# A decoder's first layer on one core: the tile experts' silu written with tanh, and the order of a recurrence's exponentials, loads and scatters

## The chip, the core and the metric

The kernel runs on one core of one Trainium2 chip. A core has TensorE (PE, matrix products and transposes), VectorE (DVE), ScalarE (ACT), GpSimd (POOL) and SyncE (SP, which only issues DMAs here); each runs its own instructions in order and waits for the others by semaphores. Products land in PSUM, everything else lies in SBUF. The metric is the device time of one execution in microseconds (us), as the median of a few runs.

## The reference

A decoder of two layers on x of 16 sequences × 128 tokens × 256 channels, all float32. The change lies in layer 0 and in the early part of layer 1:

```python
x = x + L0_attn(layernorm(x))           # 16 heads of 128, causal
x = x + L0_xattn(k=layernorm(x), v=ctx) # recurrence over the 128 tokens, per channel
x = x + L0_ffn(layernorm(x))            # 16 experts, 4 per token, and a shared expert
x = x + L1_attn(layernorm(x))
x = x + L1_xattn(layernorm(x), ctx)
x = x + L1_ffn(layernorm(x))            # weights and activations rounded
```

The recurrence carries (aa, bb, pp) from token to token and has four exponentials per token:

```python
q = max(pp, u + k);   e1 = exp(pp - q);       e2 = exp(u + k - q)
y = (e1 * aa + e2 * v) / (e1 * bb + e2)
q2 = max(pp + w, k);  e1b = exp(pp + w - q2); e2b = exp(k - q2)
aa, bb, pp = e1b * aa + e2b * v, e1b * bb + e2b, q2
```

An expert is `(silu(h @ w_gate) * (h @ w_up)) @ w_down`, with silu(g) = g · sigmoid(g), which is also 0.5 · g · (1 + tanh(g / 2)).

## The kernel before

The work is laid out for PE, whose order is the program's own in the stages below. The other engines' instructions are ordered at build time by a scheduler; `tc.issue_after(ins)` adds an edge that puts what is issued under it behind `ins` on the engine of `ins`.

**Layer-0 attention, 0 to about 610 us.** 64 units, each four heads of one sequence; 16 units make a group g of four sequences. In each step, `pipeline` runs `scores` (products into `sc`, L587; ACT copies them scaled, L589; POOL masks, L590; then the softmax with its maxima on DVE, L187, and four exponentials on ACT, L190), `values` (L625), `ahead` (the next heads' projections `proj`, L577, read out by ACT as qT and kT, L579; in one step per group POOL also adds a bias row to all of a group's x, L570), `project_out` (L175), `turn` (transposes of the probabilities, copied as `probT`, L203) and `between`.

**The recurrence beside it.** When a group's attention is done, `wkv_and_route(g)` is queued as a generator. `between` advances it by `take` with a credit of 20 per unit; each `yield` states a cost (UNIT is 15, SMALL 3). `wkv` goes through two blocks k of 128 channels: a load of vT, the context's values (L285, 256 KB, on ACT's queue), running maxima on DVE, two exponentials e1b and e2b (L295, L298), running sums aa and bb by scans, two exponentials in place of pp and q (L312, L314), and the quotient, transposed back and added to x. `route` then takes the router's choices of the group: for each token and each of its four experts a row number, first as float `fidx` and then as integers `idx` (L520, one copy per group). The 16 scatters of a group (L527, indirect DMAs issued by POOL, each 128 rows) wait in a list; `some_scatters` issues them, two per unit.

**Shared expert, about 620 to 753 us.** 24 units of `sh_hidden`, `sh_down` and `advance`. `advance(u)` runs the last group's recurrence and routing (it has no attention beside it), then `tile_map` and the first two fetches, with the edge behind `sh_hidden.last`, the unit's DVE product. SP's queue here holds the loads of the shared expert's weights, then the experts' weights (`wbig`, `wd`).

**Experts, about 753 to 1016 us.** 79 tiles j of 128 rows. Step s: `fetch`, `turn_in(s-2)` (transpose `pht`, L954, copied to `hxT` by ACT), `inner(s-3)` (product `pgu`, L970, gate and up in one PSUM tile; silu on ACT, L975; times up on DVE, L977), `turn_act(s-5)` (`pat`, L984), `outer(s-6)` (`pey`, L993) and `beside(s)`. The four PSUM tiles of a step come from one pool of four. From s = FIRST = 36 on, every second step, `beside` issues pieces of layer 1's self attention from three tables, among them its exponentials (L1168).

Of the kernel before, what the change touches and what calls it, by code (L numbers as in the profile page):

```python
# [12 lines left out]
AF = mybir.ActivationFunctionType  # L13
ALU = mybir.AluOpType
# [3 lines left out]
P = 128  # L18
# [4 lines left out]
G = 4  # L23
NG = B // G
GT = G * S
# [6 lines left out]
IMOE = 176  # L32
# [20 lines left out]
def decoder(ctx, tc, a, out):  # L53
    nc = tc.nc
    V, A, PE, GP = nc.vector, nc.scalar, nc.tensor, nc.gpsimd
# [13 lines left out]
    def ps4(name, pool="main"):  # L69
        return pools[pool].tile([P, 4, P], F32, tag="ps", name=name)  # L70
# [113 lines left out]
    def softmax(pool, sc, p):  # L184

        nmax = pool.tile([P, 4], F32, tag="nmax", name="nmax", bufs=3)
        softmax.last = V.tensor_reduce(nmax, sc, AX.X, ALU.max, negate=True).ins  # L187
        rs = pool.tile([P, 4], F32, tag="rsum", name="rsum", bufs=4)
        for i in range(4):
            A.activation(p[:, i, :], sc[:, i, :], AF.Exp, bias=nmax[:, i : i + 1], accum_out=rs[:, i : i + 1])  # L190
        return rs

    def normalised(p, rs):
# [34 lines left out]
    def flat(v):  # L228
        return v.rearrange("p t s -> p (t s)")
# [16 lines left out]
    UNIT, SMALL = 15, 3  # L246

    def take(steps, credit, unit=UNIT):
# [7 lines left out]
                credit -= cost  # L256
        return min(credit, 0)

    def wkv(g, psum):

        if not wpad:
            with tc.issue_after(softmax.last):
                wkv.wneg = wkv_setup()
        wneg = wkv.wneg
        mv, rstd = norm_stats(wkp, g)
        kp = [wkp.tile([P, G, SP], F32, tag=f"kp{k}", name=f"kp{k}") for k in range(NK)]
        yield 6
        hs = norm_rows(wkp, g, mv, rstd)
        yield UNIT
        with tc.issue_after(behind[0]):  # L270
            norm_T(hs, lambda k: kp[k][:, :, 1:], psum)
        yield 3
        for k in range(NK):

            def padded(tag, first):
                r = wkp.tile([P, G, SP], F32, tag=tag, name=tag)
                if first is not None:
                    GP.memset(r[:, :, 0:1], first)
                return r, r[:, :, :S], r[:, :, 1:]

            def plain(tag):
                return wkp.tile([P, G, S], F32, tag=tag, name=tag)

            vT = plain("vT")
            nc.scalar.dma_start(flat(vT), a["ctxT"][k * P : (k + 1) * P, g * GT : (g + 1) * GT])  # L285
            GP.memset(kp[k][:, :, 0:1], NEG)
            kt = kp[k][:, :, 1:]
            u = tfirst[:, k : k + 1]
            pp, pp0, pp1 = padded("pp", None)
            V.tensor_tensor_scan(flat(pp), flat(wpad[k]), flat(kp[k]), NEG, ALU.add, ALU.max)  # L290
            yield 3

            e1b, e1b0, e1b1 = padded("e1b", 0.0)
            V.scalar_tensor_tensor(e1b1, pp0, wneg[:, k : k + 1], pp1, ALU.add, ALU.subtract)
            A.activation(e1b1, e1b1, AF.Exp)  # L295
            e2b, bb0, e2b1 = padded("e2b", 0.0)
            GP.tensor_tensor(e2b1, kt, pp1, ALU.subtract)
            A.activation(e2b1, e2b1, AF.Exp)  # L298
            yield 2
            ev, aa0, ev1 = padded("ev", 0.0)  # L300
            GP.tensor_tensor(ev1, e2b1, vT, ALU.mult)
            q = plain("q")
            V.scalar_tensor_tensor(q, kt, u, pp0, ALU.add, ALU.max)
            yield 13

            V.tensor_tensor_scan(flat(ev), flat(e1b), flat(ev), 0.0, ALU.mult, ALU.add)
            yield 3
            V.tensor_tensor_scan(flat(e2b), flat(e1b), flat(e2b), 0.0, ALU.mult, ALU.add)
            yield 3

            GP.tensor_tensor(pp0, pp0, q, ALU.subtract)
            A.activation(pp0, pp0, AF.Exp)  # L312
            V.scalar_tensor_tensor(q, kt, u, q, ALU.add, ALU.subtract)
            A.activation(q, q, AF.Exp)  # L314
            yield 10
            GP.tensor_tensor(vT, q, vT, ALU.mult)
            V.tensor_tensor(bb0, pp0, bb0, ALU.mult)
            yield 4
            V.tensor_tensor(bb0, bb0, q, ALU.add)
            yield 2  # L320
            V.tensor_tensor(aa0, pp0, aa0, ALU.mult)
            V.tensor_tensor(aa0, aa0, vT, ALU.add)
            yield 4
            for t in range(G):
                V.reciprocal(bb0[:, t], bb0[:, t])
                yield 3
            y = q
            V.tensor_tensor(y, aa0, bb0, ALU.mult)
            yield UNIT
            pb = ps4("addb", psum)  # L330
            with tc.issue_after(behind[0]):
                for t in range(G):
                    PE.transpose(pb[:, t, :], y[:, t, :], ident)
            cols = slice(k * P, (k + 1) * P)
            V.tensor_tensor(xg[g][:, :, cols], xg[g][:, :, cols], pb, ALU.add)
            yield 3
# [8 lines left out]
    idx = rt.tile([P, B, TOPK], I32, name="idx")  # L345
# [63 lines left out]
    def route(g, psum):  # L409
# [8 lines left out]
        tiles = slice(g * G, (g + 1) * G)  # L418
# [21 lines left out]
        nmax = small("rmax", [P, G])  # L440
# [5 lines left out]
        rs = small("rrs", [P, G])  # L446
# [55 lines left out]
        for t in range(G):  # L502
            b = g * G + t
# [13 lines left out]
        V.tensor_tensor(both, pick, over_k(place_), ALU.mult)  # L517
        fidx = small("fidx", [P, G, TOPK])
        V.tensor_reduce(fidx, both, AX.X, ALU.add)
        V.tensor_copy(idx[:, tiles, :], fidx)  # L520
        yield SMALL
        V.tensor_tensor(both, pick, over_k(comb), ALU.mult)
        V.tensor_reduce(wts[:, tiles, :], both, AX.X, ALU.add)

        def scatter(t, k):
# [4 lines left out]
            tc.declare_no_dep(ins, group="hs", reason="no two tokens of an expert have one place")  # L530
            tc.add_to_no_dep_group("hs", ins)

        for t in range(G):
            for k in range(TOPK):
                scatters.append((scatter, t, k))
        yield SMALL

    def wkv_and_route(g, psum):
        yield from wkv(g, psum)
# [273 lines left out]
    def advance(u):  # L813

        behind[:] = last_pe
        with tc.issue_after(sh_hidden.last):
            advance.credit = take(steps, advance.credit, 10 if u % SHJ == 0 else 17)
        if u == 0:
            advance.power = power.last
        if u >= 2:  # L820
            some_scatters(4, advance.power)
# [137 lines left out]
    def inner(j):  # L959
        if j % NB == 0:  # L960
            _, vals = nc.values_load_multi_w_load_instructions(
                tmapT[0:1, 0, j : j + NB], engines=[ET], min_val=0, max_val=E - 1,
                skip_runtime_bounds_check_because=why,
            )
            for i, v in enumerate(vals):
                held[j + i] = v
        hT = live[j]
        pg = tps.tile([P, 2 * IMOE], F32, tag="t", name="pgu")
        for k in range(NK):
            PE.matmul(  # L970
                pg, hT[:, k, :], wgu[:, k, bass.ds(held[j], 1), :].rearrange("p e i -> p (e i)"),
                start=k == 0, stop=k == NK - 1,
            )
        s = mp.tile([P, IMOE], F32, tag="esilu", name="esilu", bufs=2)
        inner.last = A.activation(s, pg[:, :IMOE], AF.Silu).ins  # L975
        act = mp.tile([P, IMOE], F32, tag="eact", name="eact")
        softmax.last = V.tensor_tensor(act, s, pg[:, IMOE:], ALU.mult).ins  # L977
        live[j] = act

    def turn_act(j):  # L980
# [226 lines left out]
    early = ([(sa_out_T, 3)], [(sa_exponents, 4)], [(sa_values, 4)], [(sa_back, 4), (sa_norm_T, 6)])  # L1207
    late = ([(sa_project, 5), (sa_again, 4), (sa_out, 3)], [], [], [(sa_scores, 5)])
    last = ([(row_stats, 6)], [(sa_scale, 6)], [(sa_rows, 6), (sa_split, 5)], [])
# [3 lines left out]
    def pieces(table, u):  # L1213
        b, n = divmod(u, NKV)
        for f, ahead in table[n]:
            if 0 <= b + ahead < B - apart.get(f, 0):
                f(b + ahead)
# [22 lines left out]
    LAG, FIRST, APART = 6, 36, 2  # L1240
# [3 lines left out]
    def beside(s):  # L1244
        for _ in range(3):
            if s >= 1 and chores:
                chores.pop(0)()
        if s == FIRST + 6:
            assert not chores
            rawstack.close()  # L1250
            prepared()
        b, r = divmod(s - GATHER, TOPK)
        if r == 0 and 0 <= b < B - 2:
            back_rows(b)
        b, r = divmod(s - GATHER - 6, TOPK)
        if r == 0 and 0 <= b < B:
            back_sums(b)
        u, r = divmod(s - FIRST, APART)
        if r == 0 and 0 <= u < LEAD:
            u -= LEAD  # L1260
            for table in (early, late, last):
                pieces(table, u)
            for f, b, at in first_pieces:
                if u == at:
                    f(b)
        if s == NTILES + 2:
            load_weights()

# [395 lines left out]
```

## Time and profile before

| | |
|---|---|
| median of 3 runs | 1672.91 us (1672.89 to 1674.83) |
| profiled execution | 1670.1 us |
| its span, first to last instruction | 1668.4 us |
| mean granted clock of TensorE | 0.993 |
| ACT table loads: L723, L1168, L975 | 7, 4, 4 of 1283 ns each |
| vT loads, L285 | 8, issue 334 ns (median) |
| exponential of the recurrence, e.g. L314 | 128x512, 0.63 us |
| scatter, L527 | 64, 1009 ns mean |

A row of the profile names the line, the engine, the operation and the tile it writes "<-" those that it reads, then the shape. "Idle before <-releaser" tells how long the engine stood before the instruction and what ended that. A table load is ACT's change from one set of functions to another. PEld is PE's weight load, which runs beside its products. "remote" and "issue" stand where no instruction of the core is seen to have ended the wait.

### The profile page before, as it was taken

What the parts mean: (1) busy time and instruction counts of PE and PEld (TensorE: products, weight loads), DVE (VectorE), ACT (ScalarE), POOL (GpSimd) and SP (SyncE); (2) the same over time, 40 slices, a digit from 0 to 9 for tenths busy, and PEclk for the clock granted to TensorE, in tenths of its full rate; (3) what the DMA queues carried; (4) which work ended last, traced back from release to release, by engine and by line L of the source; (5) the groups of instructions that cost most, each with busy time, mean ns of one, the idle gap of its engine ahead of it and who ended that gap; (6) DMA issues with size and microseconds to landing.
All of it is one profiled execution on the core that took longest, in us unless ns stands there. A gap on an engine that the chain in (4) does not pass through costs nothing.

```text
span 1668.4 us, 27303 instructions
## 1 busy us (share of the span) xinstructions
PE 1615.0 (97%) x9808; PEld 1145.4 (69%) x9808; DVE 947.5 (57%) x2490; ACT 815.4 (49%) x2211; POOL 571.5 (34%) x586
## 2 busy tenths in 40 slices
PE   8999999999999989999999999999999999999997
PEld 4666666666666665656766667777777777777774
DVE  2333476457537656633354555567666666666756
ACT  3444454444445433303434445656666666665554
POOL 2010132144024233031364345654444444432331
PEclk9999999999999999999999999999999999999998
DMA  9990000000001028034443234000000000000000
GB/s 298 404 370 1 0 7 7 14 26 27 0 20 38 7 83 230 1 103 133 141 146 102 89 92 168 17 14 11 8 8 7 8 8 8 8 8 10 4 4 13
DMA packets 92205, 110.22 MB, mean 66 GB/s; under 512 B 8679, under 2 KB 67495, under 8 KB 92071
## 3 DMA queue, kind: packets, MB, share of 16 engines
q1 hardware_dynamic: 83638, 89.55, 16.5%
q0 software_dynamic: 6144, 16.79, 3.1%
q10 hardware_dynamic: 2288, 2.14, 0.4%
q8 instruction: 78, 1.28, 0.3%
q14 instruction: 57, 0.46, 0.1%
HBM read 54.06 MB, written 54.39 MB: 65 GB/s over the span
## 4 chain that ended last, share of the span: by engine, by line
PE 85%; DVE 6%; issue 3%; ACT 3%; POOL 2%; DMA 0%; SPq 0%; POOLq 0%; another core or an unknown queue 0%; DVEq 0%; ACTq 0%
PE proj L577 12%; PE acc_x L1433 6%; PE proj L1367 6%; PE acc_l L175 6%; PE projv L596 5%; PE pgu L970 5%; PE pey L993 4%; PE sc L1398 3%; PE z L1418 3%; PE sc L587 3%; PE z L625 3%; PE pg L717 2%; PE acc_sh L736 2%; PE pk L1333 2%; PE pu L717 2%
## 5 line engine op out<-in xcount | busy, mean ns | idle before, releaser
L190 ACT ACTIVATE sc<-sc,nmax 128x128 f32<-128x128 f32 x512 | 199.0, 390 | 162.2 <-DVE nmax L187 132.4
L187 DVE TENSOR_REDUCE nmax<-sc 128x4 f32<-128x512 f32 x128 | 87.3, 682 | 159.5 <-POOL sc L590 157.9
L590 POOL TENSOR_SCALAR_AFFINE_SELECT sc<-sc 128x512 f32<-128x512 f32 x64 | 42.1, 658 | 317.1 <-ACT sc L589 317.1
L1367 PEld LDWEIGHTS proj<-hc,wbig 128*128 128x128 f32 x1024 | 124.0, 192 | 29.2 <-issue 23.4
L125 POOL TENSOR_TENSOR rq<-rq,mhalf 128x4 f32<-128x4 f32 x64 | 67.8, 1059 | 210.4 <-DVE rq L1390 194.2
L577 PE MATMUL proj<-hT,wq 128*128 128x512 f32 x256 | 122.5, 601 | 4.3 <-DVE probT L203 3.9
L1433 PE MATMUL acc_x<-wbig,zT 128*128 128x256 f32 x512 | 124.6, 386 | 0.7 <-ACT zT L1424 0.7
L1367 PE MATMUL proj<-hc,wbig 128*128 128x128 f32 x1024 | 124.6, 275 | 0.1
L175 PEld LDWEIGHTS acc_l<-wo,zT 128*128 128x128 f32 x512 | 96.7, 190 | 36.8 <-issue 26.5
L577 PE MATMUL proj<-hT,wk 128*128 128x512 f32 x256 | 120.9, 595 | 0.0
L175 PE MATMUL acc_l<-wo,zT 128*128 128x256 f32 x512 | 120.9, 379 | 0.0
L596 PE MATMUL projv<-wv,hT 128*128 128x512 f32 x256 | 120.6, 593 | 0.0
L970 PE MATMUL pgu<-wbig,hxT 128*128 x316 | 109.0, 468 | 1.8 <-DVE eactT L986 0.5
L1433 PEld LDWEIGHTS acc_x<-wbig,zT 128*128 128x128 f32 x512 | 93.4, 190 | 24.0 <-issue 11.5
L125 POOL TENSOR_TENSOR ss<-ss,mhalf 128x32 f32<-128x32 f32 x16 | 87.6, 5477 | 45.0 <-DVE ss L1116 44.8
L1227 POOL DMA_INDIRECT back<-hs,idx x64 | 64.3, 1005 | 94.2 <-DMA hs<-ey 40.7
L190 ACT ACTIVATION_READ_ACCUMULATOR sc<-sc,nmax 128x1 f32 x512 | 95.6, 187 | 0.0
L1401 DVE SCALAR_TENSOR_TENSOR sc<-sc,rq,mask 128x128 f32<-128x128 f32 x256 | 77.5, 344 | 28.2 <-PE sc L1398 24.7
L577 PEld LDWEIGHTS proj<-hT,wk 128*128 128x128 f32 x256 | 49.1, 192 | 62.1 <-issue 53.2
L986 DVE COPY eactT<-pat 88x256 f32<-88x256 f32 x79 | 33.0, 418 | 101.4 <-PE pat L984 82.3
L625 PEld LDWEIGHTS z<-probT,v 128*128 128x128 f32 x512 | 66.9, 191 | 31.8 <-issue 27.0
L993 PE MATMUL pey<-wd,eactT 88*128 x316 | 82.0, 381 | 1.6 <-ACT hxT L956 0.9
(349 smaller groups left out, 3501.0 us busy)
## 6 DMA issues: line engine op xcount, KB each, us to landing
hs<-zero SPq DMA_DIRECT2D x16, 2048.0 KB
hx<-hs SPq DMA_DIRECT2D x79, 128.0 KB
hs<-ey SPq DMA_DIRECT2D x79, 128.0 KB
wbig<-in_L_ffn_w_gate_dram SPq DMA_DIRECT2D x2, 1408.0 KB
wbig<-in_L_ffn_w_up_dram SPq DMA_DIRECT2D x2, 1408.0 KB
wd<-in_L_ffn_w_down_dram SPq DMA_DIRECT2D x2, 1408.0 KB
wq<-in_L_attn_W_Q_dram SPq DMA_DIRECT2D x8, 256.0 KB
vT<-in_ctxT_dram ACTq DMA_DIRECT2D x8, 256.0 KB
```

Source lines behind the costliest of these rows:

```text
L125: power.last = GP.tensor_tensor(v, v, mhalf[:, :n], ALU.pow).ins
L175: ins = PE.matmul(acc[:, t, :], zT[:, i, :], w[:, h0 + i, :], start=h0 == 0 and i == 0 and t % 2 == 0, stop=last and i == 3, skip_group_ch ...
L187: softmax.last = V.tensor_reduce(nmax, sc, AX.X, ALU.max, negate=True).ins
L190: A.activation(p[:, i, :], sc[:, i, :], AF.Exp, bias=nmax[:, i : i + 1], accum_out=rs[:, i : i + 1])
L577: PE.matmul(pj, w[:, k, h, :], hTs[g][:, k, :], start=k == 0, stop=k == NK - 1)
L596: PE.matmul(pv, hTs[g][:, k, at], wv[:, k, 4 * hq : 4 * hq + 4, :].rearrange("p h e -> p (h e)"), start=k == 0, stop=k == NK - 1,)
L625: PE.matmul(pz[:, i, :], v[:, i, :], pT[:, i, :], start=True, stop=True)
L970: PE.matmul(pg, hT[:, k, :], wgu[:, k, bass.ds(held[j], 1), :].rearrange("p e i -> p (e i)"), start=k == 0, stop=k == NK - 1,)
L993: ins = PE.matmul(py, aT[:, k, :], wd[:, bass.ds(held[j], 1), k, :].rearrange("p e d -> p (e d)"), start=k == 0, stop=k == 1,)
L1367: PE.matmul(pj[:, i, :], wqx[:, n, k, i * DH : (i + 1) * DH], hTs[b][:, k, :], start=k == 0, stop=k == NK - 1,)
L1401: V.scalar_tensor_tensor(sc[:, i, :], psc[:, i, :], rq[:, i : i + 1], mask, ALU.mult, ALU.add)
L1433: PE.matmul(accs[b][:, :D], zT[:, i, :], wox[:, 4 * n + i, :], start=n == 0 and i == 0, stop=n == NKV - 1 and i == 3,)
```

## The change

- The four exponentials of the recurrence get an edge behind the last exponential of the current unit's softmax (`softmax.exps`, `exp_behind`), and the cost stated after the last of them is 14 and not 10.
- vT is loaded by SP's queue and not by ACT's.
- The integer copy of the row numbers is made per tile, each with its four scatters behind it and a yield of UNIT between (UNIT // 2 for the last group).
- `advance(0)` has no edge behind the unit's product.
- In tiles j ≥ FIRST − 4 = 32 silu is tanh(g/2) on ACT and two DVE instructions, (tanh + 1) · g and 0.5 · that · up; before, it was a silu on ACT and one product on DVE.
- The layer-1 pieces in `beside` are issued under an edge behind the tile's activation.

```diff
+        softmax.exps = ins.ins
...
+    def exp_behind(v):
+
+        with tc.issue_after(softmax.exps):
+            A.activation(v, v, AF.Exp)
...
-            nc.scalar.dma_start(flat(vT), a["ctxT"][k * P : (k + 1) * P, g * GT : (g + 1) * GT])
+            nc.sync.dma_start(flat(vT), a["ctxT"][k * P : (k + 1) * P, g * GT : (g + 1) * GT])
...
-            A.activation(e1b1, e1b1, AF.Exp)
+            exp_behind(e1b1)
...
-            A.activation(e2b1, e2b1, AF.Exp)
+            exp_behind(e2b1)
...
-            A.activation(pp0, pp0, AF.Exp)
+            exp_behind(pp0)
             V.scalar_tensor_tensor(q, kt, u, q, ALU.add, ALU.subtract)
-            A.activation(q, q, AF.Exp)
-            yield 10
+            exp_behind(q)
+            yield 14
...
-        V.tensor_copy(idx[:, tiles, :], fidx)
-        yield SMALL
...
+        yield SMALL
         for t in range(G):
+            V.tensor_copy(idx[:, g * G + t, :], fidx[:, t, :])
             for k in range(TOPK):
                 scatters.append((scatter, t, k))
-        yield SMALL
+            yield UNIT if g < NG - 1 else UNIT // 2
...
-        with tc.issue_after(sh_hidden.last):
+        with tc.issue_after(sh_hidden.last) if u else ExitStack():
             advance.credit = take(steps, advance.credit, 10 if u % SHJ == 0 else 17)
...
-        inner.last = A.activation(s, pg[:, :IMOE], AF.Silu).ins
         act = mp.tile([P, IMOE], F32, tag="eact", name="eact")
-        softmax.last = V.tensor_tensor(act, s, pg[:, IMOE:], ALU.mult).ins
+        if j < FIRST - 4:
+            inner.last = A.activation(s, pg[:, :IMOE], AF.Silu).ins
+            softmax.last = V.tensor_tensor(act, s, pg[:, IMOE:], ALU.mult).ins
+        else:
+
+            inner.last = A.activation(s, pg[:, :IMOE], AF.Tanh, scale=0.5).ins
+            V.scalar_tensor_tensor(s, s, 1.0, pg[:, :IMOE], ALU.add, ALU.mult)
+            softmax.last = V.scalar_tensor_tensor(act, s, 0.5, pg[:, IMOE:], ALU.mult, ALU.mult).ins
...
-            for table in (early, late, last):
-                pieces(table, u)
-            for f, b, at in first_pieces:
-                if u == at:
-                    f(b)
+
+            with tc.issue_after(inner.last):
+                for table in (early, late, last):
+                    pieces(table, u)
+                for f, b, at in first_pieces:
+                    if u == at:
+                        f(b)
```

## The prediction

> **What bounds the kernel now.** I read the page's header first, then the chain that ended last, then what TensorE (PE) waited for, then the timeline around the longest of those waits.
>
> ```profile
> span 1668.4 us, 27303 instructions
> PE 1615.0 (97%) x9808; PEld 1145.4 (69%) x9808; DVE 947.5 (57%) x2490; ACT 815.4 (49%) x2211; POOL 571.5 (34%) x586
> PE 85%; DVE 6%; issue 3%; ACT 3%; POOL 2%; DMA 0%; SPq 0%; POOLq 0%; another core or an unknown queue 0%; DVEq 0%; ACTq 0%
> ```
>
> PE is busy for 1615.0 of 1668.4 us. None of its products is removed, so the change can win only from the other 53.4 us. By the windows of the trace, 7.3 of them lie in the start, about 6 in the layer-0 attention between 200 and 540, 7.3 between 600 and 640, 3 in the shared expert after 720, 14.8 in the experts between 760 and 1060, and about 10 in the last 28 us. What ended those waits:
>
> ```profile
> PE lnT L160 <- DVE hrow L151: 8.2, 2, 6.7
> PE pht L954 <- ACT hxT L956: 6.8, 3, 2.4
> PE pg L717 <- issue: 4.7, 1, 4.7
> PE proj L577 <- DVE probT L203: 3.9, 2, 2.0
> ...
> PE z L625 <- ACT kT L579: 1.9, 2, 0.9
> PE acc_sh L736 <- issue: 1.6, 1, 1.6
> PE acc_sh L736 <- DVE act L725: 1.4, 1, 1.4
> PE pcnt L495 <- DVE gtb L491: 1.1, 1, 1.1
> ```
>
> (Columns: total us, times, longest.) The start, the 4.7 us between the stages and the tail are not touched. "proj behind probT", "z behind kT" and the short "lnT" wait are.
>
> **Exponentials behind the softmax, and vT on another queue.** The first of the two proj waits, in order of time:
>
> ```profile
> 253.51 4.59 POOL L570 TENSOR_TENSOR x<-x,bo_row 128x1024 f32<-128x1024 f32 x1 [3.96 <-DVE hrow L151]
> ...
> 258.10 1.26 POOL L316 TENSOR_TENSOR vT<-q,vT 128x512 f32<-128x512 f32 x1
> 259.40 0.69 DVE L322 TENSOR_TENSOR ev<-ev,vT 128x512 f32<-128x512 f32 x1 [3.50 <-POOL vT L316]
> 260.00 0.68 DVE L203 COPY probT<-pT 128x512 f32<-128x512 f32 x1
> 260.12 0.33 ACTq L285 DMA_DIRECT2D vT<-in_ctxT_dram  x1
> 260.56 0.60 ACT L589 ACTIVATE sc<-sc 128x512 f32<-128x512 f32 x1 [5.23 <-DVE ev L322]
> 260.74 0.30 PEld L577 LDWEIGHTS proj<-hT,wq 128*128 128x128 f32 x2 [2.10 <-DVE probT L203]
> ```
>
> The bias add of 4.59 us on POOL delays the product of L316; DVE stands 3.50 us for it with the copy probT behind; PE waits for that copy. Meanwhile ACT stands 5.23 us, because the next vT load sits in its queue and needs the old vT to be free; the softmax's score copy is behind it. The same picture comes back at 415.23. The unit is 9.10 us of PE; the excess of each unit over that (after the unit's own transposes) gives 2.08 us at 260.74, 2.12 at 415.23, 1.21 at 376.26 and 1.20 at 530.74 (there the exponentials of L312 and L314 stand before kT on ACT), and 0.4 in small ones: **7.0 us** in all. The change attacks both: vT goes to SP, which has little else to issue here, so ACT's order is only arithmetic; the exponentials follow the unit's softmax exponentials instead of standing before qT and kT; and the changed program's order, as built, puts the probT copy of that unit on ACT and not on DVE behind L322. POOL's 4.59 us add stays, still in front of a score mask (L590) with L286 and L316 between them: the mask can start at 259.4 where it started at 261.23. Between 0 (the waits form again one unit later, since the recurrence is as long as it was) and 7.0 us I take **5.0**: the four large waits are 6.6, and a quarter of that comes back. Each vT load is one issue of 0.33 us, now on SP. Its first stands before the 16 zeroing stores and six stand before the shared expert's weights; each waits for the vT before it, the latest of these for a product at about 570 us, well before the weights' own release near 616. The eighth stands behind the experts' weights (wbig, wd): in the trace it was issued at 657.81 and POOL waited 1.9 us for it. Behind 8.4 MB of weights it could come up to some 10 us later; that stage has slack of 14 us (the first tile's fetch at 739.06, the stage's end near 753), so 0 here, and up to 3 if the routing's last steps slip.
>
> **Scatter tile by tile.** One index copy per group becomes four (12 more DVE instructions, about 0.1 us each, 1.2 us beside PE), and the 16 scatters of a group become due four at a time. The scatters are 1.0 us each on POOL, off PE's path. The pcnt wait of 1.1 us ends on DVE's gtb, which moves a unit with its consumer: 0, bounds −1 to +1.
>
> **First shared unit freed.** At u = 0 the vector work of the recurrence no longer has to follow the first act. The second lnT wait, 1.5 us at 636.78, ended with statistics queued behind that act. I give 1.0 of it, and 0.2 of the 1.6 and 1.4 us after 730, whose late vector copies the map's reordering moves: **1.2 us**, bounds 0 to 4.5.
>
> **Tanh for silu in tiles 32 to 78 (47 tiles).** Removed: the table loads between silu and the pieces' exponentials. ACT has them as follows:
>
> ```profile
> 967.59 1.28 ACT L1168 ACT_TABLE_LOAD   x1
> ...
> 971.23 1.28 ACT L975 ACT_TABLE_LOAD   x1
> ```
>
> Eight go (four at L975, three of four at L1168, the one before layer 1's first exponential at 1032.60). Each is 1.283 us, in sum 10.3 us of ACT. The Trainium skill ("ScalarE: Activation LUTs", What ACT_TABLE_LOAD costs) puts 1283 ns plus a drain of about 1380 ns on a switch, 2.66 us: 21.3 us for eight. The trace agrees with the load, but the load at 967.59 starts 0.03 us after the ACTIVATE before it ended, and the next ACTIVATE starts at 968.88: no drain shows, so I use 1.283. Of it PE sees little: about 0.14 and 0.22 us of waits follow the two loads of each of the four blocks of pieces, 4 × 0.36 = **1.4 us**. At 1032.60 ACT stands a further 0.26 us for the row maximum after its load: hidden, 0.
>
> Added: a second DVE instruction per tile.
>
> ```profile
> L975 ACT ACTIVATE esilu<-pgu 128x176 f32<-128x176 f32 x79 | 25.2, 319 | 53.4 <-PE pgu L970 48.1 <-issue 3.3 <-PE pat L984 1.1
> L977 DVE TENSOR_TENSOR eact<-esilu,pgu 128x176 f32<-128x176 f32 x79 | 25.4, 325 | 3.5 <-ACT esilu L975 3.4
> ```
>
> (Busy us and mean ns, then the idle time before.) The nearest row of its kind, L1517, is 583 ns for 416 columns; with the 325 ns of 176 columns as the other point, the form costs about 0.33 us at this width. 47 × 0.33 = 15.5 us of DVE, where DVE is busy 71.0 of the 136 us from 880 to 1016: room enough. What counts is the path product, tanh, two vector steps, release of the PSUM bank. Comparing the end of each eact with the start of the next product, 46 tiles of 830 to 1012 leave mostly 0.2 us or more, but 11 of them 0.01 or less, as PE's step waits there already. If each of the 11 pays 0.33 us, that is 3.6; the tanh tiles with no such delay pay nothing. Here the skill speaks against the change: "VectorE: DVE Perf Modes" (The DRAIN you can't avoid) adds a drain of duration minus 266 ns after each vector instruction, that is 0.07 us per step, and 11 × 0.40 = 4.4. The trace shows the next vector instruction starting before the end of the last (259.40 + 0.69, then 260.00), so 3.6 is the end I keep. Between 0 and 3.6 I take **2.0** lost, since part of the late eacts come from the ACT delay that the missing loads shorten.
>
> The pieces' edge behind the tile's activation orders ACT alone; the pieces are later than the tile there and their own work is the same: 0, bounds ±1.
>
> **Sum.** −5.0 −1.2 −1.4 +2.0 = −5.6 us. The profiled execution took 1670.1 (span 1668.4 and 1.7 around it); it would take 1664.5. The median of the runs is 1672.9, 2.8 above it, so I forecast 1672.9 − 5.6 = **1667.3 us**. Its own range, with 3 to 9.5 us gained, is 1663.4 to 1670.
>
> **Rivals.**
> - *The waits move and do not go.* POOL's 4.59 us add and the 15 or so POOL and DVE steps of the recurrence are all still there, and a reordered ACT only shifts the unit that meets them. For: the add still precedes a score mask. Against: ACT's 5.23 us stand is caused by the vT load alone. Then 1.5 of the 7.0 return, the tanh part is even: 1.5 + 1.0 = 2.5 gained, 1670.4.
> - *The expert step becomes bound by the PSUM release (slower).* If each of the 47 tiles, not 11, pays the 0.33 us, +15.5, less 5.0 + 1.2 + 1.4: +7.9, 1680.8. It decides from the point where the slack of 0.2 us after an eact is the true slack: records of a product start up to 0.27 us before the eact it should wait for ended, so the slack is more probably 0.5, and 0.33 fits. Speaking for it: 25 of the 46 tiles leave less than 0.33.
> - *All waits named go*: 7.0 + 1.5 + 3.0 + 1.4 = 12.9 gained, nothing paid by the tiles: 1660.
>
> **Chances.** Forecast 0.56, waits move 0.16, PSUM release 0.16, all go 0.12. A measurement of this kernel can tell about 0.2% from no change, 3.3 us: faster is below 1669.6. All of the last case lies there, 0.49 of the forecast's 0.56 and 0.05 of the rival whose waits move: faster 0.66. What is left of these two is within 0.2%, but for 0.01: 0.17. Slower is the PSUM release and that 0.01: 0.17. The range 1659 to 1677 leaves out most of the slower case and little else.
>
> **What would show it.** The unit excesses at 260.7 and 415.2 gone or below 0.5 us, and the ACT wait "sc behind ev" of 10.4 us gone, show the first step right; a new wait of the mask or of probT one unit later shows it wrong. Sixteen table loads in place of 24. In the experts, product waits ending on eact, or the time of the 47 tiles longer by over 4 us, show the slower rival. Vector steps of the last group ending after 753 would show the eighth vT load late. The forecast is wrong if the attention stage, up to about 610, is not shorter by at least 3 us.

## The result, and the profile after

The kernel became slower: 1675.45 us median (1673.13 to 1681.78, 20 runs) against 1671.17 (1663.10 to 1674.83, 20 runs) before, a ratio of 1.0035 with a 95% interval of 1.0026 to 1.0044. (Ratios here are estimated from all the runs; the quotient of these two medians is 1.0026.) The forecast was 1667.3 us and a gain of 5.6; measured is a loss of 4.3. On two other chips the loss was 12.4 us (ratio 1.0078, 1.0064 to 1.0092) and 7.4 us (1.0041, 1.0026 to 1.0057). The profiled execution after, at 1681.8 us, is the slowest of its 20, so it serves to find waits and not to add them up.

The header of the page after, and its chain by engine:

```profile
span 1680.1 us, 27380 instructions
PE 1623.7 (97%) x9808; PEld 1151.5 (69%) x9808; DVE 964.9 (57%) x2545; ACT 807.6 (48%) x2207; POOL 566.3 (34%) x586
PE 84%; DVE 7%; issue 3%; POOL 3%; ACT 1%; another core or an unknown queue 1%; DMA 0%; SPq 0%; POOLq 0%; DVEq 0%; ACTq 0%
```

ACT became 7.8 us less busy, as eight table loads went; run 8 below shows what the tanh tiles are worth alone. What PE waited for between 190 and 760 us (total, times, longest):

```profile
PE acc_sh L743 <- DVE act L732: 8.9, 1, 8.9
PE pmap L804 <- DVE diag L798: 4.8, 1, 4.8
PE proj L584 <- ACT probT L204: 4.4, 2, 2.2
PE lnT L160 <- DVE hg L429: 2.7, 1, 2.7
PE z L632 <- ACT kT L586: 1.9, 2, 0.9
```

"proj behind probT" was to go and is longer than before (3.9); only the engine of the copy has changed. Three waits are new. The first wait of proj, in order of time (PE's weight loads left out):

```profile
254.80 1.22 DVE L312 TENSOR_TENSOR_SCAN ev<-e1b,ev 128x516 f32<-128x516 f32 x1
...
254.96 3.20 POOL L577 TENSOR_TENSOR x<-x,bo_row 128x1024 f32<-128x1024 f32 x1 [3.96 <-DVE hrow L151]
...
255.94 3.31 DVE L314 TENSOR_TENSOR_SCAN e2b<-e1b,e2b 128x516 f32<-128x516 f32 x1
...
259.17 0.72 DVE L319 SCALAR_TENSOR_TENSOR q<-kp,L_xattn_time_first,q 128x512 f32<-128x512 f32 x1
...
259.92 0.63 ACT L263 ACTIVATE q<-q 128x512 f32<-128x512 f32 x1 [4.85 <-DVE q L319]
...
260.46 0.57 ACT L204 COPY probT<-pT 128x512 f32<-128x512 f32 x1
...
261.08 1.98 PE L584 MATMUL proj<-hT,wq 128*128 128x512 f32 x4 [2.17 <-ACT probT L204]
```

The recurrence is a step behind where it was: its second scan (L314) now meets POOL's bias add. That scan takes 3.31 us where the first one, just before, took 1.22, and it ends 1.1 us after the add. This fits the Trainium skill ("SBUF — State Buffer", SBUF: two separate sides), by which a DVE instruction with two SBUF inputs and a POOL instruction that reads SBUF exclude each other for their whole length; the rows show the delay, not the lock. ACT then waits 4.85 us with q's exponential ahead of the copy probT. The new edge is not what puts it there: run 9 has the same order without it.

The longest wait, in the shared expert's first units:

```profile
620.00 1.06 POOL L531 DMA_INDIRECT hs<-hg,idx  x1 [7.40 <-DVE idx L540]
...
628.12 0.17 DVE L137 TENSOR_SCALAR rstd<-bnmv 128x4 f32<-128x4 f32 x1
...
639.09 0.96 POOL L531 DMA_INDIRECT hs<-hg,idx  x1 [0.30 <-issue]
640.08 1.04 POOL L125 TENSOR_TENSOR rstd<-rstd,mhalf 128x4 f32<-128x4 f32 x1
641.16 1.38 DVE L151 TENSOR_SCALAR hrow<-x,bnmv,rstd 128x256 f32<-128x256 f32 x4 [12.87 <-POOL rstd L125]
642.46 1.27 DVE L732 TENSOR_TENSOR act<-silu,pu 128x512 f32<-128x512 f32 x2
643.19 3.57 PE L743 MATMUL acc_sh<-wsh,act 128*128 128x256 f32 x8 [8.92 <-DVE act L732]
```

Before, the same scatters and power stood so:

```profile
610.40 1.06 POOL L527 DMA_INDIRECT hs<-hg,idx  x1 [4.01 <-DVE idx L520]
...
629.50 0.96 POOL L527 DMA_INDIRECT hs<-hg,idx  x1 [0.30 <-issue]
...
635.23 1.05 POOL L125 TENSOR_TENSOR rstd<-rstd,mhalf 128x4 f32<-128x4 f32 x1 [4.76 <-DVE rstd L137]
```

Group 2's 16 scatters, 1.27 us apart, were over before the power was due, and the power waited for DVE. Here they start at 620.00 and not at 610.40, the power's input is ready at 628.3, and the power waits behind them until 640.08. DVE stands 12.87 us for it, and the acts of units 0 and 1 (L732), which PE needs, stand behind.

### The profile page after: what moved, and what is told of

The parts are those of the page before. It is cut to its first block, busy times and chain, and to the rows that moved or that the text cites. A ratio compares the mean times of both kernels' runs of the same rounds, so it can differ in the third digit from the quotient of the medians.

```text
span 1680.1 us, 27380 instructions
## 1 busy us (share of the span) xinstructions
PE 1623.7 (97%) x9808; PEld 1151.5 (69%) x9808; DVE 964.9 (57%) x2545; ACT 807.6 (48%) x2207; POOL 566.3 (34%) x586
## 4 chain that ended last, share of the span: by engine, by line
PE 84%; DVE 7%; issue 3%; POOL 3%; ACT 1%; another core or an unknown queue 1%; DMA 0%; SPq 0%; POOLq 0%; DVEq 0%; ACTq 0%
PE proj L584 12%; PE acc_x L1448 6%; PE proj L1382 6%; PE projv L603 5%; PE acc_l L175 5%; PE pgu L977 5%; PE sc L1413 3%; PE pey L1006 3%; PE sc L594 3%; PE z L1433 3%; PE z L632 3%; PE acc_sh L743 2%; PE pg L724 2%; PE pk L1348 2%; PE pu L724 2%
```

## The experiments

Lengths of stages are compared between chips only where the text says so. The kernel before took 1652.7, 1652.3, 1666.7 and 1666.4 us on the chips of the four sets (runs 1 to 4, 5 to 8, 9 to 12, 13 to 16); each ratio is to runs on its own chip.

**Run 1, the changed kernel again.** No edit.

> The changed kernel itself, a second profile. If its new waits are its own (theory A: the scatters of group 2 start about 10 us later, POOL's power for the last group's norm stands behind them, and the freed first unit puts that norm ahead of the first act on DVE), the wait of acc_sh for act near 643 is again 6 us or more, and the map's wait near 749 again 3 us or more. If they were an accident of one execution (theory B), both are under 2 us here. Ratio to the kernel before 1.0035 within 0.002.

1665.08 us, ratio 1.0078 (1.0064 to 1.0092). The wait of acc_sh was 8.9 us again, so it is no accident. The map's wait of 4.8 was absent; it came back (4.5) in run 13. The ratio was further from 1 than expected. Run 5, on a chip where the kernel before takes the same time, shows that kernel without its 4.7 us wait between the stages (0.8), so there this wait does not offset the loss.

**Run 2, the first shared unit tied again.**

```diff
-        with tc.issue_after(sh_hidden.last) if u else ExitStack():
+        with tc.issue_after(sh_hidden.last):
```

> The changed kernel, with the edge behind the first shared unit's act put back. Theory A: the acts of units 0 and 1 no longer stand behind the norm, so acc_sh starts some 8 us earlier; but the norm's power is still behind 16 scatters that end near 640, so the transposes lnT wait in its place: 3 to 8 us gained of the 8.9 plus one or two stretches of half clock, ratio to before 0.998 to 1.001. Theory C (the shared stage only shifts a delay that the DMA loads set): no gain, 1.0035.

1662.26 us, 2.8 less than run 1, ratio 1.0058 (1.0044 to 1.0071). As foreseen, lnT waits 5.6 us in place of acc_sh's 8.9; the ratio fell short of the expected one, so most of the loss lies elsewhere. Freeing the unit is a loss of 2.8 us here.

**Run 3, one index copy per group.**

```diff
+        V.tensor_copy(idx[:, tiles, :], fidx)
         yield SMALL
...
-            V.tensor_copy(idx[:, g * G + t, :], fidx[:, t, :])
...
-            yield UNIT if g < NG - 1 else UNIT // 2
+        yield SMALL
```

> The changed kernel, with one index copy per group and the scatters listed at once, as before. Theory A: the first scatter of group 2 is near 611 and not 620, so the power near 630 is free, and the wait of acc_sh falls from 8.9 to under 3 us; the map comes earlier too, so its wait of 4.8 us falls below 2. 8 to 14 us gained with the half clock that follows such waits: ratio 0.996 to 0.999. Theory C: the delay stays, 1.002 to 1.004. If the cost lies in the tanh tiles (theory D), this stays above 1.002.

1663.63 us, ratio 1.0072 (1.0058 to 1.0085); the 1.4 us below run 1 are within the spread of both. The first scatter still came at 618.9 and acc_sh still waited 8.5 us. My theory of where the delay comes from fell here: the copies by tile are not what makes the scatters late.

**Run 4, silu kept.**

```diff
-        if j < FIRST - 4:
+        if j < NTILES:
...
-            with tc.issue_after(inner.last):
+            with ExitStack():
```

> The changed kernel, with silu in all 79 tiles and the pieces without the edge. In the two traces the stretch from tile 24 to the last product of the experts took 209.4 us before and 207.6 after, so theory A takes the tanh part for a gain of about 2 us and expects this kernel slower than the changed one by 1 to 3 us: ratio to before 1.004 to 1.006. Theory D (the tanh tiles cost, as the prediction had it with 2.0 us less 1.4): faster than the changed one by 0.6 us or more, up to 3.6: ratio 1.001 to 1.003.

1663.21 us, 1.9 less than run 1, ratio 1.0065 (1.0051 to 1.0078). The size is as theory D had it, but the runs of both overlap, and the runs below do not bear it out.

**Run 5, the kernel before, profiled on a quick chip.** No edit.

> The kernel before, a profile on the chip of these runs. Its median here is 1652.7 against 1671.2 on the first chip: theory F (the difference between the chips is in stretches that the change does not touch, the transfers and waits of the experts and of the shared expert's end) expects the attention stage equal within 1 us to the first profile (last acc_l near 619.6), and the stretch from tile 24 to the last product below 200 us, where it was 209.4. If the attention stage differs by over 3 us, the profiles of the two chips cannot be compared stage by stage.

1652.37 us. The last acc_l is at 620.2, within a microsecond of the first profile; tile 24 to the last product took about 198 us, against 209.4 there. So the chips differ after the attention, and the attention can be compared. What PE waits for between 190 and 760:

```profile
PE proj L577 <- DVE probT L203: 3.8, 2, 2.0
PE lnT L160 <- DVE hrow L151: 2.3, 1, 2.3
PE z L625 <- ACT kT L579: 1.8, 2, 0.9
PE pcnt L495 <- DVE gtb L491: 1.1, 1, 1.1
PE pg L717 <- DVE x L640: 0.8, 1, 0.8
```

**Run 6, the yield of 10.** In the changed kernel, one number:

```diff
-            yield 14
+            yield 10
```

> The changed kernel with the cost after the last exponential at 10 again and not 14. Theory A2 (this yield, not the index copies, makes group 2's recurrence end one unit later, so that routing meets the short units at the stage's end): the counts pcnt near 604 and not 614.6, the scatters from 611, the power of the last group near 631, the wait of acc_sh for act under 4 us in place of 8.9, the wait lnT behind hg under 1.5 in place of 2.7; 6 to 11 us gained of the 12.4 that the change costs here: ratio 1.001 to 1.004. Rival G (the edges behind the softmax delay the recurrence by a unit by themselves): pcnt stays at 614, ratio 1.006 to 1.008.

1651.71 us, ratio 0.9992 (0.9983 to 1.0001): the whole of the 12 us is gone. Its waits in the same stretch:

```profile
PE acc_sh L743 <- DVE act L732: 6.0, 1, 6.0
PE z L632 <- ACT kT L586: 1.9, 2, 0.9
PE pcnt L501 <- DVE gtb L497: 1.1, 1, 1.1
```

Against run 1, proj's 4.4 and lnT's 2.7 us are gone, and the gain is larger than expected, since the two waits of proj go as well. Only acc_sh fell short: 6.0 and not under 4. The last scatter ends at 625.02 and the power follows at 625.03, so it still stands behind the scatters. Around POOL's bias add it runs as the prediction drew it:

```profile
252.73 4.59 POOL L577 TENSOR_TENSOR x<-x,bo_row 128x1024 f32<-128x1024 f32 x1 [3.96 <-DVE hrow L151]
...
254.44 0.57 ACT L204 COPY probT<-pT 128x512 f32<-128x512 f32 x1
...
257.37 1.88 PE L584 MATMUL proj<-hT,wq 128*128 128x512 f32 x4
...
258.54 0.62 POOL L597 TENSOR_SCALAR_AFFINE_SELECT sc<-sc 128x512 f32<-128x512 f32 x1
```

The copy is done long before proj needs it. Group 2's counts (pcnt) are at 598.1 (run 1: 614.6; run 5: 604.4), its first scatter at 605.0 (618.8; 611.0).

**Run 7, the exponentials free, with the yield of 10.**

```diff
-            exp_behind(e1b1)
+            A.activation(e1b1, e1b1, AF.Exp)
```

and so for the other three.

> The changed kernel without the edges behind the softmax's exponentials, and with the yield of 10. If the edges cost nothing beside the yield, equal to the kernel with the yield of 10 alone within 1.5 us. If they delay the recurrence (rival G), this one alone has pcnt near 604 and a ratio of 1.001 to 1.004. The waits proj behind probT of 2.2 us (at 260 and 416) stay within 0.5 us if POOL's bias add and the scan beside it set them, and go if the exponential of q ahead of the copy probT on ACT does.

1651.91 us, ratio 1.0000 (0.9990 to 1.0009). The same as run 6: the edges themselves neither cost nor gain, and pcnt is at 598.6.

**Run 8, tanh alone.** The kernel before with the tanh tiles and the pieces' edge.

> The kernel before with the tanh tiles and the pieces' edge alone. Keeping silu in the changed kernel gained 1.9 us, so theory D (the longer path from product to the release of its PSUM bank) expects this one slower than before by 1 to 3 us: ratio 1.0006 to 1.002. Theory H (the silu kernel's gain was a different course of the clock and of the transfers after 1000, not the tiles) expects no loss or a gain of 1 to 2 us: 0.999 to 1.000.

1652.98 us, ratio 1.0000 (0.9992 to 1.0009): theory H, no loss and no gain.

**Run 9, the yield of 14 alone.** In the kernel before:

```diff
-            yield 10
+            yield 14
```

> The kernel before with the one cost after the last exponential at 14 and not 10, nothing else. Theory A2 (this number is what costs: group 2's routing slips a unit into the short units at the end of the attention, its scatters then stand before the last group's power) expects pcnt near 614, first scatter near 619, the wait lnT behind hg of 2.7 us, a wait of 5 us or more in the shared expert's first units, and a ratio of 1.004 to 1.007. Rival G2 (it costs only together with the edges or with vT on SP): below 1.002.

1666.85 us, ratio 1.0004 (0.9985 to 1.0024). The profile had all that was expected (pcnt at 615.6, first scatter at 619.4, waits of 2.7 and 5.3 us), the time did not. The 35 runs of the kernel before on this chip spread from 1660 to 1671, so the ratio does not decide. The waits of proj are those of the changed kernel, 4.7 us in two:

```profile
255.86 3.31 DVE L308 TENSOR_TENSOR_SCAN e2b<-e1b,e2b 128x516 f32<-128x516 f32 x1
...
259.84 0.63 ACT L314 ACTIVATE q<-q 128x512 f32<-128x512 f32 x1 [5.37 <-DVE q L313]
...
261.00 1.98 PE L577 MATMUL proj<-hT,wq 128*128 128x512 f32 x4 [2.30 <-ACT probT L203]
```

This kernel has no edges on the exponentials and its vT load on ACT's queue: the cost of 14 makes this picture by itself.

**Run 10, vT alone.** The kernel before with one line changed:

```diff
-            nc.scalar.dma_start(flat(vT), a["ctxT"][k * P : (k + 1) * P, g * GT : (g + 1) * GT])
+            nc.sync.dma_start(flat(vT), a["ctxT"][k * P : (k + 1) * P, g * GT : (g + 1) * GT])
```

> The kernel before with vT loaded by SP's queue, nothing else. Theory J (the two waits proj behind probT of 1.9 us, and the half clock after one of them, came from the vT load in ACT's queue alone; both kernels with the yield of 10 and vT on SP lost them, with the exponentials' edges and without) expects units 32 and 48 to start as in the kernel with the yield of 10, the last acc_l near 614, and 4 to 7 us gained: ratio 0.9955 to 0.9975. Rival K (the tile-wise index copies or the freed first unit also had a part in it): at most 2 us gained, above 0.9985.

1659.55 us, 7.1 less than before, ratio 0.9959 (0.9939 to 0.9979). Theory J: both waits of proj are gone and the last acc_l is at 614.9. The copy probT is on ACT in this build, at 255.16, although POOL's add takes 4.60 us as before.

**Run 11, the yield of 10 and the first unit tied.** The changed kernel with the edits of runs 2 and 6.

> The changed kernel with the yield of 10 and the first shared unit tied again: the parts that are left are the edges, vT on SP, the index copies by tile and the tanh tiles. Theory A: the wait of 5.96 us of acc_sh becomes the 2.35 us of lnT that the kernel before has, with one stretch of half clock less: 3 to 5 us gained against the kernel with the yield of 10, ratio 0.996 to 0.998. Rival L (the freed first unit is no cost, since POOL's power comes after the scatters in either case): 0.998 to 1.000.

1656.75 us, ratio 0.9946 (0.9925 to 0.9967): faster than the kernel before, and more than theory A had expected. acc_sh no longer waits in the first units, and lnT waits 0.8 us.

**Run 12, vT and two scatters per unit.** Run 10's kernel, and

```diff
-            some_scatters(2 if u < NG * NQ * G - 4 else 4, last_pool[0])
+            some_scatters(2, last_pool[0])
```

> As the one with vT on SP alone, and in the attention's last units two scatters per unit in place of four, so that 8 of group 2's 16 stand behind the last group's power on POOL and not before it. Theory A: the power comes near 620, the wait lnT behind hrow of 2.35 us and the half clock after it go, 2 to 4 us gained against vT on SP alone: ratio 0.993 to 0.9955. Rival M (the wait is set by the statistics on DVE or by the first act, not by POOL): same as vT on SP alone within 1 us.

1663.04 us, ratio 0.9988 (0.9967 to 1.0009), not better than vT alone. The power came at 625.4 (run 10: 629.8) and lnT waited no longer, but the other eight scatters now stood in front of the recurrence's own products on POOL:

```profile
636.66 0.96 POOL L533 DMA_INDIRECT hs<-hg,idx  x1 [0.30 <-issue]
...
637.64 1.29 POOL L303 TENSOR_TENSOR e2b<-kp,pp 128x512 f32<-128x512 f32 x1
...
640.89 2.19 DVE L312 TENSOR_TENSOR_SCAN ev<-e1b,ev 128x516 f32<-128x516 f32 x1 [6.64 <-POOL ev L307]
...
645.34 1.99 PE L742 MATMUL acc_sh<-wsh,act 128*128 128x256 f32 x8 [2.93 <-DVE act L731]
```

The wait moved on, to acc_sh.

**Run 13, the changed kernel once more**, beside the next three.

> The changed kernel beside the next three on one chip. If the chip is one where the kernel before takes about 1652, ratio 1.006 to 1.009; if about 1667 to 1671, where the kernel before has waits of its own between the stages, 1.002 to 1.005.

1673.76 us, ratio 1.0041 (1.0026 to 1.0057).

**Run 14, the yield of 14 alone, again.** The edit of run 9.

> The kernel before with the yield of 14 alone, once more. Theory A2 (the number costs by itself; the first measurement of it lay on a chip where runs of the kernel before spread from 1660 to 1671 and hid it): within 3 us of the changed kernel on the same chip, as its waits in the first profile were the same ones. Rival G2 (it costs only with vT on SP or the freed unit): more than 5 us faster than the changed kernel and within 2 us of before.

1669.29 us, ratio 1.0022 (1.0002 to 1.0042). Both theories missed: it is 2.9 us above before and 4.5 below the changed kernel. So the number costs something by itself here, just clear of the interval, and the rest of the loss comes with the other parts: lnT waits 5.3 us here where acc_sh waits 8.9 in run 13, and the map's wait of 4.5 is run 13's alone. Which part makes the map late is not shown.

**Run 15, the yield of 10 and the first unit tied, again.** The kernel of run 11.

> The changed kernel with the yield of 10 and the first unit tied, once more: it was 0.9946 of before on the spread chip. Theory A expects 0.994 to 0.998 on any chip, and 8 us or more between it and the changed kernel.

1654.98 us, ratio 0.9927 (0.9906 to 0.9948): 11.4 us faster than before, more than expected, and 18.8 faster than the changed kernel. Its first shared units:

```profile
624.39 0.96 POOL L531 DMA_INDIRECT hs<-hg,idx  x1 [0.30 <-issue]
...
625.07 0.24 DVE L137 TENSOR_SCALAR rstd<-bnmv 128x4 f32<-128x4 f32 x1
...
625.47 1.05 POOL L125 TENSOR_TENSOR rstd<-rstd,mhalf 128x4 f32<-128x4 f32 x1
625.85 1.89 PE L743 MATMUL acc_sh<-wsh,act 128*128 128x256 f32 x8
626.55 1.38 DVE L151 TENSOR_SCALAR hrow<-x,bnmv,rstd 128x256 f32<-128x256 f32 x4 [1.23 <-POOL rstd L125]
627.58 1.04 PE L160 MATMUL lnT<-ident,hrow 128*128 128x128 f32 x8
```

The last scatter ends at 625.35, the power follows 0.12 us later, the act is ahead of the norm, and PE waits for neither.

**Run 16, the same with silu.** Runs 15 and 4 together.

> The same with silu in all tiles and the pieces without the edge. Theory D (the tanh tiles cost about 2 us): 1 to 3 us faster than the one with tanh. Theory H (tanh is even, as it was alone, 1.0000): within 1 us of it.

1658.85 us, ratio 0.9952 (0.9934 to 0.9970). The one with tanh is 3.9 us faster, against theory D, but the intervals meet.

## Why the prediction was wrong

**The step that failed is the −5.0 us of the exponentials and vT**, and in it a term that was missing: the prediction set out the load's queue and the order on ACT, and gave the change of the cost from 10 to 14 no price at all. Two blocks per group make 8 more cost units, and a unit of attention takes 20. So the generator slips (pcnt at 604.4 in run 5, at 615.6 with this number alone in run 9), and by run 6 that number was worth the whole loss: 13.4 us between runs 1 and 6, on two chips where the kernel before takes the same time within 0.4 us. Compared at the same milestones on the quick chips:

| | run 5, before | run 1, changed | run 6, yield of 10 |
|---|---|---|---|
| last acc_l | 620.2 | 624.7 | 613.9 |
| second group of the shared expert | 654.8 | 666.8 | 652.9 |
| first tile of the experts | 749.9 | 760.9 | 747.3 |
| span | 1650.7 | 1662.1 | 1650.0 |

The change lost 4.5 us in the attention and 7.5 in the first shared units, and got 1.0 back until the experts. The two parts act together:

| waits of proj, total us | vT on ACT's queue | vT on SP's queue |
|---|---|---|
| cost of 10 | 3.8 (run 5) | none (runs 6, 7, 10) |
| cost of 14 | 4.7 (run 9) | 4.4 (run 1) |

So half of the prediction's mechanism is right at the yield of 10. Moving the load removes the waits of proj (run 10 does it with that line alone), and the attention is 6.3 us shorter in run 6 where 5.0 was said, 1.7 of it, by estimate, a stretch of half clock that goes too (last section). The other half, the exponentials behind the softmax, did nothing: runs 6 and 7 are equal. The first rival (the waits move and do not go) named what happened, but for another reason: it took the steps to meet the same unit in another order, and they meet another unit. The two waits of 0.9 us of z behind kT, counted among the four large ones, never went in any run.

**The second wrong step is the −1.2 us of the freed first unit.** Run 2 shows +2.8. I took the norm behind the act for the loss; but DVE works in order, and a norm put ahead of the act carries its own wait, for POOL, into the act.

**The scatters and the pcnt wait at 0** missed too. The pcnt wait of 1.1 us went and lnT behind hg came at 2.7, so +1.6 where −1 to +1 was the bound. In run 5 DVE starts the statistics for hg at 584.25, right behind the sum into x at 583.52; in run 1 the sum is at 585.03, the statistics come behind the next unit's maxima, at 587.86, and PE waits. With the cost of 14 alone (run 9) it waits the same 2.7. The scatters, put off PE's path, are on it: PE waits for what stands behind the power, and the power stands behind 16 of them.

**The tanh tiles, −1.4 + 2.0.** The sizes of the rows were right: 326 and 333 ns for the two steps where 0.33 us was said, and 16 loads for 24. The sum of +0.6 is compatible with what was measured: 0 alone (run 8), +1.9 (run 4 against 1) and −3.9 (run 16 against 15). No sign is settled. The slower rival, a release of PSUM that costs 15.5 us, is excluded by run 8: that a loss was on the list of rivals is luck, as it came from elsewhere.

**The eighth vT load** behind the experts' weights, up to 3 us, cost nothing that PE shows: in run 6 no wait of PE between 640 and 760 is over 0.4 us.

What is not settled: why on three chips PE, DVE and SP stand still for some us between the stages (4.7 before, 3.4 in run 10, 2.8 in run 15) and near 730 (4.0 in run 15), where the two others show 0.8 and nothing. The map's wait, seen in the changed kernel on two of these chips, may be of this kind: DVE stands 7.74 us before it, and no instruction of the core is seen to end that. The kernels that come to the first place later wait 0.8 there too (the changed kernel on the first chip, runs 9, 13 and 14), which offsets part of their loss. The yield of 14 alone was not run on a quick chip, and neither was the kernel of runs 11 and 15: how much of its 11.4 us would remain there is open. Run 6 was not repeated on the first chip.

## What to carry to other kernels

Where side work is paced by stated costs, a cost is a position: a change of one number moves every later step of that work against the main loop, so lay the new schedule beside the old one, unit by unit, and see which long instruction of another engine each step will meet. When a change has several parts, test them apart: here one line, the load's queue, was worth 7.1 us (run 10), and a number beside it undid that. A step that depends on a slow queue should stand behind the work that the busiest engine waits for, not ahead of it, even if it is long due.

## What the runs showed of the hardware that was not expected

A wait of PE cost more than its length. The trace's record of the granted clock shows half clock in stretches of 3.41 us or a multiple; between 190 and 760 us each comes during a wait of PE or soon after. In the profile after, the eight products of acc_sh at 643.19 take 3.57 us in such a stretch; in run 15 they take 1.89. Windows of 20 us of run 5, run 1 and run 15, whose PE is busy throughout (busy time of PE, its weight loads, DVE, ACT and POOL, then the granted clock, DMA share and GB/s):

```profile
640.00:660.00 20.00, 20.00 (x81) 11.81 (x80) 14.42 (x19) 9.20 (x11) 5.04 (x6) 1.00 0.85 194
```

```profile
580.00:600.00 20.00, 17.29 (x86) 13.24 (x85) 9.88 (x26) 7.06 (x21) 2.32 (x3) 0.91 0.00 1
...
640.00:660.00 20.00, 18.09 (x54) 11.66 (x55) 9.50 (x14) 7.38 (x9) 4.80 (x3) 0.80 0.95 250
```

```profile
620.00:640.00 20.00, 20.00 (x65) 11.61 (x64) 10.67 (x22) 7.59 (x11) 9.84 (x9) 0.99 1.10 345
```

Run 1 has 54 rows of products between 640 and 660 where run 5 has 81. Between 190 and 760 us run 5 has two such stretches of 3.41 us (from 415.1 and 633.6) and run 1 five (from 415.7, from 593.2, and three on end from 637.6). What of them lies outside the waits is 6.8 us in run 5 and 12.6 in run 1. If half of it is lost, 2.9 of the 11.0 us that run 1 is behind at the experts' start are this, by estimate. The Trainium skill ("TensorE: Matmul & The Clock Gate", Part 1: The HAM clock gate) has the gate close after an idle window of about 3.4 us that runs freely. The runs agree with the length of the stretches. Waits shorter than a window, though, were enough at times: 1.95 us near 414 in run 5 was followed by half clock from 415.1, while the same wait of 1.96 us in the first profile was not. In run 1 the wait of 2.2 us near 415 was followed by it, and the one of 2.2 us near 260 was not. What decides, such as where the window falls, is not shown. Half of a stretch, 1.7 us, is then an estimate of how far apart two executions of one kernel can be by one such wait.
